# Moving the pace of layer 0 and the choice of engine for tanh rows in a two-layer attention kernel

## The chip, the cores and the metric

The kernel runs on one core of a Trainium2 chip. The metric is the device time of one execution in microseconds (us). The median of three runs of the kernel before is 5696.39 us (5690.69 to 5700.09).

## What is computed

The input x is 8 batches of 1024 tokens with 128 channels. Two layers follow each other.

```
# layer 0, 8 heads
q, k, v = x @ wq.T + bq, x @ wk.T + bk, x @ wv.T + bv
scores  = q . k / sqrt(128)                    # 1024 x 1024 for each batch and head; tokens (m, g) = 64 x 16
a       = softmax(softmax(scores, over m), over g)
x1      = layer_norm(a @ v @ wo.T + bo + x)
x2      = layer_norm(relu(x1 @ w1.T + b1) @ w2.T + b2 + x1)
# layer 1
B       = layer_norm(x2);  Wi = B @ W.T
s[i, j] = sum over d of v[d] * tanh(Wi[i, d] + Wi[j, d])
t       = x2 + softmax(s) @ B
out     = t + recurrence(layer_norm(t))        # y = sigmoid(wx_t + y @ V.T) along the tokens
```

Within a batch, layer 1 needs all of layer 0. Different batches are independent up to the recurrence, which takes its normalisation from all of them.

## The kernel before, in words

Everything but the opening loads and the closing recurrence is put down as a list of small operations, each with the engines that may do it and its cost there, its dependencies, and a priority (`pri`, a number: lower goes first). `Plan.emit` then plays the list through: it keeps a planned time for every engine, looks at the operations whose dependencies are planned, takes those that could start within 0.15 us of the earliest, and among these emits the one with the lowest sum of priority and the engine's own handicap. The instructions of each engine stand in the program in that order, which is fixed; on the chip an engine works through its own order and waits where it must. An operation that more than one engine may do goes to the one that wins this choice.

**Layer 0 of a batch** (`layer0(b)`) goes over 8 heads and, in a head, over 8 tiles of 128 queries. For each tile: scores on PE (L856), exponential on ACT (L859), sums over m and reciprocals on DVE (L863, L864), division on DVE (L867). For each pair of tiles: second exponential on ACT (L876, 2048 elements per partition), sums and reciprocals on DVE (L879, L880), division on GpSimd (POOL, L890), transposes on PE with copies by DVE (L770, L782), the product with the values on PE (L904) and its addition to zs on DVE (L909, L911). There are two score buffers (sc), two pairs of tile buffers (e) and two transposed buffers (aT). After the last head come a norm, the feed-forward matmuls (L944, L957) and another norm. The priority of a tile is its place on a pace line: `b - 1 - LEAD + STRETCH * (share of layer 0 done)`, with LEAD = 0.15 and STRETCH = 0.95 (1.25 for the last batch), so 64 tiles are 0.95/64 apart. In the first and last batch layer 0 is done in two halves of queries. In batch 0 nothing else is there to do beside it, and ACT may do evictions as well.

**Layer 1 of a batch** (`layer1(b)`) norms the tokens and projects them to wiT (L1085, copied by DVE, L782 and L1109). Scores are symmetric, so of the 8 x 8 blocks of 128 x 128 only the 36 on and over the diagonal are computed: row block `it` has `8 - it` of them. A *group* is one step of such a row block: tanh of the sums of `4k` tokens with all later ones, in one of five th buffers, and its product with v on PE (L1062, times_v). k is 1 for the wide row blocks 0 to 3, 2 for 4 and 5, and 4 and 8 for 6 and 7. A group can be filled in three ways:

- ACT alone: one activation per token with the token as bias (L999);
- POOL adds (L1009, four instructions over k tokens), then ACT makes one tanh of the whole buffer (L1045);
- DVE adds: row by row where k < 4 (L1003, with an accumulator output that nobody reads), or as POOL does where k >= 4 (L1009), then ACT's L1045.

The first operation of the group decides which engine fills it. The list `fillers` of `layer1` names the engines that may: for the wide row blocks ACT and POOL, and DVE in the last batch only. The priority of the rows of batch b goes from b to b + 0.222 (ROWS); their matmuls come LEAD ahead of that. The exponentials of the scores (L1158), transposes and the product with B (L1191) follow. The rest of layer 1 has priority b - 0.5. The parked outputs and wx go out and come back by SP's DMA queue.

The last stage is the recurrence (L1372 to L1381), and the transposed sums with the parked outputs.

```
def pace(n_part, h):
    return b - 1 - LEAD + STRETCH * (n_part * H + h) / (len(parts) * H)
...
ROWS = b + (past + n_blocks * s / 33) / len(E_first) / 4.5
L1 = ROWS - LEAD
```

Of the kernel before, what the change touches and what calls it, by code (L numbers as in the profile page):

```python
# [413 lines left out]
class Plan:  # L414
# [24 lines left out]
    def add(self, where, fn, r=(), w=(), pri=0, mode="full", take=None, give=None, behind=(), wait=(), port=False):  # L439
        n = len(self.ops)  # L440
        deps = set()
        for k in r:
            if k in self.writer:
                deps.add(self.writer[k])
        for k in (*w, *wait):
            if k in self.writer:
                deps.add(self.writer[k])
            deps.update(self.readers.get(k, ()))
        for k in w:
            self.writer[k] = n  # L450
            self.readers[k] = []
        for k in r:
            if k not in w:
                self.readers.setdefault(k, []).append(n)
        deps.discard(n)
        self.ops.append((where, fn, (pri, n), mode, deps, take, give, behind, port))
        self.by.append(None)
        return n
# [107 lines left out]
def fast_path(ctx: ExitStack, tc: tile.TileContext, a: dict, fits):  # L566
# [6 lines left out]
    NB, N, C = a["x"].shape  # L573
# [143 lines left out]
    add = plan.add  # L717


    LEAD, SOON, LATE = 0.15, 0.5, -0.3  # L720

    stats = ring("stat", 7, [P, 4, 9])

# [36 lines left out]
    def through_bank(pe, weight, r, evict, where, more, w, pri, choice=two):  # L760

        bank = Bank(*choice)
        n = len(plan.ops)
        add(("PE", weight), lambda _: pe(bank()), r=r, w=[("bank", n)], pri=pri, take=bank, wait=more + w)
        add(where, lambda e: evict(e, bank()), r=[("bank", n)] + more, w=w, pri=pri, give=bank)

    def transposes(srcs):
        def fn(bank):
            for i, s in enumerate(srcs):
                nc.tensor.transpose(bank[:, i * P : (i + 1) * P], s, ident)  # L770

        return fn

    def copy(dst):
        def fn(e, bank):
            src = bank
            if len(dst.shape) == 3:
                src = bank[:, : dst.shape[1] * P].rearrange("p (t c) -> p t c", c=P)
            if e == "ACT":
                nc.scalar.activation(dst, src, AF.Copy)  # L780
            else:
                nc.vector.tensor_copy(dst, src)  # L782

        return fn
# [4 lines left out]
    def layer0(b):  # L789
# [13 lines left out]
        def pace(n_part, h):  # L803
            return b - 1 - LEAD + STRETCH * (n_part * H + h) / (len(parts) * H)

        for n_part, part in enumerate(parts):
# [3 lines left out]
            for h in range(H):  # L810
                L0 = pace(n_part, h)
# [29 lines left out]
                for qt in qts:  # L841
                    L0 = pace(n_part, h + (qt - qts[0]) / len(qts))
# [30 lines left out]


                    ks = [("e", pair, q) for q in range(2)]
                    add(("ACT", 1.9), lambda _, e2=e2: nc.scalar.activation(e2, e2, AF.Exp), r=ks, w=ks, pri=L0)  # L876

                    def second_sums(_, e2=e2, r2=r2):
# [42 lines left out]
            L0 = b - 1 - SOON  # L921
# [53 lines left out]

    def group(it, at0, r0, k, wiT, all_wi, L1, ROWS, fillers, chain, left, both, first_half):

# [80 lines left out]
        def times_v(_):  # L1058
# [15 lines left out]
            ("PE", k * (1.69e-3 * (w - begin[0]) + 0.005 * n)), times_v, r=[("tanh", g)] + before,  # L1074
            w=[("sa", it, r0)] + after, pri=L1, mode="groups", give=slot,
        )
        return ("sa", it, r0)

    def projected(src, ks, w, use, kw, L1, bT, kb):

        through_bank(
            transposes([src[:, i, :] for i in range(4)]), 0.52, ks, copy(bT), ("DVE", 0.7), [], [kb], L1
        )
        through_bank(
            lambda bank: nc.tensor.matmul(bank, w, bT, start=True, stop=True), 0.9, [kb], *use, [], [kw], L1  # L1085
        )
# [8 lines left out]
    def layer1(b):  # L1095
        L1 = b - SOON
        X, kX = Xs[b % NX], ("X", b % NX)
        B, kB = Bs[b % 2], ("B", b % 2)
        wiT, kw = wiTs[b % 2], ("wiT", b % 2)

        early = b in (0, NB - 1)
        for qh in (1, 0) if early else (0, 1):
            Xg, kg = X[:, 4 * qh : 4 * qh + 4, :], kX + (qh,)
            Bg = B[:, 4 * qh : 4 * qh + 4, 0:C]
            layer_norm(Xg, kg, Bg, kB + (qh,), 6, L1)

            def numbered(_, bank, qh=qh):
                dst = wiT[:, 512 * qh : 512 * qh + 512]
                nc.vector.tensor_copy(dst.rearrange("p (t r c) -> p t r c", t=4, c=4), bank.rearrange("p (t c r) -> p t r c", t=4, c=4))  # L1109


            at = wiT[:, 512 * qh : 512 * qh + 512]
            projected(Bg, [kB + (qh,)], wa_sb, (numbered, ("DVE", 0.75)), kw + (qh,), L1, at, kw + (qh,))
        all_wi = [kw + (1,), kw + (0,)]

        E_at = E_first
        fills = [("fill", False), ("fill", True)]
        order = ((4,), (5, 7), (6,), (0,), (1,), (2,), (3,)) if early else shared  # L1120
        done, attended = set(), set()
        past = 0
        for pair in order:
            todo = []
            for it in pair:
                w = N - it * P
                k = max(1, N // w)
                wide = it < NT // 2
                for r0 in range(0, 32, k):
                    late = r0 + 3 * k >= 32  # L1130
                    if wide:
                        fillers = [("ACT", 0.0)] + ([] if late else [("POOL", 0.0)])
                        if b == NB - 1:
                            fillers += [("DVE", 0.1)]
                    elif it == NT // 2:
                        fillers = [("DVE", 0.1), ("ACT", 0.1)] + ([] if late else [("POOL", 0.0)])
                    else:
                        fillers = [("DVE", 0.1)] + ([("ACT", 0.1)] if early else [("POOL", 0.0)])
                    todo.append((r0 + 0.5 * (not wide), it, 0 if it == pair[0] else N - pair[0] * P, r0, k, fillers))
            left = {}  # L1140
            n_blocks = sum(NT - it for it in pair)
            keys = []
            for s, it, at0, r0, k, fillers in sorted(todo):
                ROWS = b + (past + n_blocks * s / 33) / len(E_first) / 4.5
                L1 = ROWS - LEAD
                keys.append(group(it, at0, r0, k, wiT, all_wi[:1] if early and pair[0] >= NT // 2 else all_wi, L1, ROWS, fillers, fills[it < NT // 2], left, fills if r0 == 0 else (), b == 0 and pair[0] >= NT // 2))
            past += n_blocks
            blocks = [("E", it, j) for it in pair for j in range(it, NT)]

            runs = [pair] if not early else [(it,) for it in pair]  # L1150

            def exps(_, runs=runs):
                at0 = 0
                for run in runs:
                    w = sum(NT - it for it in run)
                    Ep = E_sb[:, E_at[run[0]] : E_at[run[0]] + w, :].rearrange("p t (c r) -> p t c r", c=4)
                    S = sa[:, at0 : at0 + w * P].rearrange("p (t r c) -> p t c r", r=32, c=4)
                    nc.scalar.activation(Ep, S, AF.Exp)  # L1158
                    at0 += w * P

            add(("ACT", 0.2 * len(runs) + 0.833e-3 * n_blocks * P), exps, r=["sa"] + keys, w=blocks, pri=L1)
            for it in pair:
                D, kD = E_sb[:, E_at[it], :], ("E", it, it)
                add(("DVE", 0.28), lambda _, D=D: nc.vector.tensor_tensor(D, D, half, ALU.mult),
                    r=[kD], w=[kD], pri=L1, port=True)
                through_bank(
                    transposes([D]), 0.25, [kD],
                    lambda _, bank, D=D: nc.vector.tensor_tensor(D, bank[:, :P], D, ALU.add),
                    ("DVE", 0.3), [kD], [kD], L1,
                )  # L1170
            done.update(pair)
            for it in range(NT):
                if it not in attended and done.issuperset(range(it + 1)):
                    attended.add(it)
                    attention(b, it, X, kX, B, kB, E_at, L1)
# [67 lines left out]
    def check_bounds():  # L1243
# [73 lines left out]
        add(("DVE", 1.7), compared, r=[("at1", 0), ("at1", 1)] + [("ET", j) for j in range(1, NT)], w=["fits"], pri=LATE)  # L1317

    layer0(0)
    check_bounds()  # L1320
    for b in range(NB):
        if b + 1 < NB:
            load_xT(b + 1)
            layer0(b + 1)
        layer1(b)
# [139 lines left out]
```

## Time and profile before

| what | value |
|---|---|
| median of three runs | 5696.39 us |
| the profiled execution, its own time | 5699.62 us |
| its span, first to last instruction | 5697.8 us |
| mean granted clock of TensorE | 0.975 |
| PE busy | 5166.6 us (91%) |
| ACT busy | 5263.0 us (92%) |
| DVE busy | 4754.1 us (83%) |
| POOL busy | 4186.4 us (73%) |
| rows of one batch, first L1062 to the next batch's first, batches 1 to 4 | 680, 679, 679, 674 us |
| last feed-forward matmul of layer 0 of batch 7 (L957) | ends at 5184 us |
| last matmul of the rows of batch 7 | starts at 5601 us |

PE is TensorE's matmuls, PEld its weight loads, DVE is VectorE, ACT ScalarE, POOL GpSimd. Busy shares are averages over stages that differ: an opening of some 400 us with layer 0 of batch 0, a long stage in which layer 0 of batch b + 1 runs beside the rows of batch b, the rows of batch 7 alone, and some 97 us of recurrence and output. Durations of instructions that follow each other closely overlap, so start-to-start distances are shorter than the durations. The ends of matmuls are modelled, so a busy PE is not a PE at its peak.

### The profile page before, as it was taken

What the parts mean: (1) busy time and instruction counts of PE and PEld (TensorE: products, weight loads), DVE (VectorE), ACT (ScalarE), POOL (GpSimd) and SP (SyncE); (2) the same over time, 40 slices, a digit from 0 to 9 for tenths busy, and PEclk for the clock granted to TensorE, in tenths of its full rate; (3) what the DMA queues carried; (4) which work ended last, traced back from release to release, by engine and by line L of the source; (5) the groups of instructions that cost most, each with busy time, mean ns of one, the idle gap of its engine ahead of it and who ended that gap; (6) DMA issues with size and microseconds to landing.
All of it is one profiled execution on the core that took longest, in us unless ns stands there. A gap on an engine that the chain in (4) does not pass through costs nothing.

```text
span 5697.8 us, 97791 instructions
## 1 busy us (share of the span) xinstructions
PE 5166.6 (91%) x39013; PEld 2765.7 (49%) x39013; DVE 4754.1 (83%) x7545; ACT 5263.0 (92%) x4964; POOL 4186.4 (73%) x2678
## 2 busy tenths in 40 slices
PE   8899999899989999899998999989998999987567
PEld 6555455455544555445454455445454445543125
DVE  7989676778996889968898689986899669999886
ACT  5499999999998999899998999989998999999994
POOL 2362997788877888588796888868887886882882
PEclk9999999999999999999999999999999999998988
DMA  2000000000000000000000000000000000000001
GB/s 60 1 5 1 1 1 5 8 1 1 1 5 8 1 1 1 8 5 1 1 5 5 5 1 1 5 8 1 1 1 3 7 1 1 1 21 14 1 1 64
DMA packets 27330, 37.82 MB, mean 7 GB/s; under 512 B 2464, under 2 KB 19232, under 8 KB 26864
## 3 DMA queue, kind: packets, MB, share of 16 engines
q1 hardware_dynamic: 24832, 27.99, 1.5%
q8 instruction: 308, 5.05, 0.4%
q10 hardware_dynamic: 1872, 3.16, 0.2%
q14 instruction: 158, 1.29, 0.1%
q0 software_dynamic: 160, 0.33, 0.1%
HBM read 19.41 MB, written 12.06 MB: 6 GB/s over the span
## 4 chain that ended last, share of the span: by engine, by line
PE 40%; DVE 24%; ACT 23%; issue 4%; POOL 1%; DMA 0%; DVEq 0%; ACTq 0%; POOLq 0%
PE sa L1062 16%; ACT th L1045 10%; ACT th L999 9%; PE m L904 8%; PE sc L856 6%; PE m L770 4%; DVE th L1003 3%; DVE stat_e L879 3%; DVE th L1009 3%; DVE stat_e L863 2%; DVE aT L782 2%; ACT wx L876 2%; DVE wx L867 2%; ACT sc L859 2%; PE m L1191 1%
## 5 line engine op out<-in xcount | busy, mean ns | idle before, releaser
L1009 POOL TENSOR_TENSOR th<-wiT 128x896 f32<-128x896 f32 (+55 forms) x2088 | 3131.7, 1535 | 436.8 <-PE sa L1062 400.4
L1062 PE MATMUL sa<-th,vpat 128*32 128x512 f32 (+27 forms) x24576 | 2104.4, 466 | 223.6 <-ACT th L1045 212.6
L999 ACT ACTIVATE th<-wiT 128x516 f32<-128x516 f32 (+55 forms) x3044 | 2203.1, 798 | 37.1 <-DVE wiT L1109 21.1
L1045 ACT ACTIVATE th<-th 128x4096 f32<-128x4096 f32 (+54 forms) x766 | 2083.8, 2746 | 49.0 <-DVE th L1003 28.0
L890 POOL TENSOR_TENSOR wx<-wx,stat_e 128x1024 f32<-128x1024 f32 x512 | 998.3, 1971 | 755.9 <-DVE stat_e L880 527.5
L1062 PEld LDWEIGHTS sa<-th,vpat 128*32 128x32 f32 x24576 | 674.8, 111 | 1470.4 <-issue 834.4
L856 PE MATMUL sc<-xT,wx 128*128 128x512 f32 x2048 | 985.7, 606 | 36.0 <-DVE wx L867 35.8
L904 PE MATMUL m<-aT,wx 128*128 128x256 f32 x3584 | 862.2, 389 | 14.7 <-DVE aT L782 12.0
L1003 DVE TENSOR_SCALAR_CACHE_REDUCE th<-wiT 128x384 f32<-128x384 f32 (+47 forms) x1092 | 758.1, 694 | 86.3 <-PE sa L1062 15.0
L904 PEld LDWEIGHTS m<-aT,wx 128*128 128x128 f32 x3584 | 660.7, 191 | 238.9 <-issue 89.9
L782 DVE COPY aT<-m 128x512 f32<-128x512 f32 x927 | 598.2, 672 | 138.6 <-PE m L770 136.2
L863 DVE TENSOR_REDUCE stat_e<-sc 128x16 f32<-128x1024 f32 x512 | 620.1, 1211 | 101.1 <-ACT sc L859 99.9
L879 DVE TENSOR_REDUCE stat_e<-wx 128x128 f32<-128x2048 f32 x256 | 583.2, 2278 | 102.5 <-ACT wx L876 101.8
L867 DVE TENSOR_TENSOR wx<-sc,stat_e 128x1024 f32<-128x1024 f32 x512 | 623.4, 1218 | 23.8 <-DVE stat_e L864 0.5
L770 PE MATMUL m<-ident,wx 128*128 128x128 f32 x3932 | 571.9, 280 | 56.7 <-DVE aT L782 29.3
L770 PEld LDWEIGHTS m<-ident,wx 128*128 128x128 f32 x3932 | 434.9, 141 | 357.6 <-issue 164.2
L859 ACT ACTIVATE sc<-sc 128x1024 f32<-128x1024 f32 x512 | 513.1, 1005 | 92.3 <-PE sc L856 76.6
L876 ACT ACTIVATE wx<-wx 128x2048 f32<-128x2048 f32 x256 | 486.8, 1902 | 90.8 <-DVE wx L867 90.8
L856 PEld LDWEIGHTS sc<-xT,wx 128*128 128x128 f32 x2048 | 357.3, 192 | 367.1 <-issue 301.7
L1009 DVE TENSOR_TENSOR th<-wiT 128x1024 f32<-128x1024 f32 (+28 forms) x280 | 392.1, 1439 | 3.9 <-PE sa L1062 3.0
L880 DVE RECIPROCAL stat_e<-stat_e 128x128 f32<-128x128 f32 x256 | 243.9, 953 | 8.8
L738 POOL TENSOR_TENSOR stat<-stat,neg_half 128x4 f32<-128x4 f32 x64 | 65.3, 1020 | 245.4 <-DVE stat L735 230.6
(169 smaller groups left out, 3055.5 us busy)
## 6 DMA issues: line engine op xcount, KB each, us to landing
xT<-in_xt_dram SPq DMA_DIRECT2D x8, 512.0 KB, 3.7
th<-in_x_dram SPq DMA_DIRECT2D x8, 512.0 KB, 7.5
parked<-X SPq DMA_DIRECT2D x16, 256.0 KB, 2.3
xr<-parked SPq DMA_DIRECT2D x8, 512.0 KB, 8.3
parked_wx<-bT SPq DMA_DIRECT2D x14, 256.0 KB, 2.0
wx<-parked_wx SPq DMA_DIRECT2D x7, 512.0 KB, 3.3
out_dram<-ot ACTq DMA_DIRECT2D x8, 256.0 KB, 2.1
out_dram<-ot SPq DMA_DIRECT2D x8, 256.0 KB, 2.2
```

The lines of the kernel that those rows point to most:

```text
L770: nc.tensor.transpose(bank[:, i * P : (i + 1) * P], s, ident)
L856: nc.tensor.matmul(sc[:, cols], u[:, qt * P : (qt + 1) * P], xT[:, cols], start=True, stop=True)
L863: nc.vector.tensor_reduce(r1, sc.rearrange("p (m g) -> p g m", g=G), AX.X, ALU.add)
L867: nc.vector.tensor_tensor(e3, sc3, r1.unsqueeze(1).to_broadcast([P, M, G]), ALU.mult)
L879: nc.vector.tensor_reduce(r2, e2.rearrange("p q (m g) -> p q m g", g=G), AX.X, ALU.add)
L890: nc.gpsimd.tensor_tensor(e3, e3, r2[:, q, :].unsqueeze(2).to_broadcast([P, M, G]), ALU.mult)
L904: nc.tensor.matmul(bank()[:, :256], vp[:, t, :], aT[:, t, :], start=t == 0, stop=t == NT - 1)
L999: nc.scalar.activation(rows(c)[:, r, :], wiT[:, i0 + begin[c] :], AF.Tanh, bias=w_i(c, r))
L1003: nc.vector.tensor_scalar(rows(c)[:, r, :], wiT[:, i0 + begin[c] :], w_i(c, r), 0.0, ALU.add, ALU.add, accum_out=unused)
L1009: eng.tensor_tensor(rows(c), wiT[:, i0 + begin[c] :].unsqueeze(1).to_broadcast(shape), w_i(c).unsqueeze(2).to_broadcast(shape), ALU.add,)
L1045: lambda _: nc.scalar.activation(slot()[:, : at[4]], slot()[:, : at[4]], AF.Tanh),
L1062: nc.tensor.matmul(sa[32 * c : 32 * c + 32, s:s1], vpat[:, 31 - r0 - r : 63 - r0 - r], rows(c)[:, r, s - at0 - begin[c] : s1 - at0 - begin ...
```

## The change

Three edits. LEAD in the pace of layer 0 goes from 0.15 to 0.35; the matmuls of the rows keep 0.15 as a literal. From the second exponential of a pair on, the operations of that pair in layer 0 take a priority that is lower by DOWN = 0.06. And in the fillers of the wide row blocks DVE is named, with a handicap of 0.1, in all batches and not in the last alone.

```diff
-    LEAD, SOON, LATE = 0.15, 0.5, -0.3
+
+    LEAD, DOWN, SOON, LATE = 0.35, 0.06, 0.5, -0.3
...
                     ks = [("e", pair, q) for q in range(2)]
+                    L0 -= DOWN
                     add(("ACT", 1.9), lambda _, e2=e2: nc.scalar.activation(e2, e2, AF.Exp), r=ks, w=ks, pri=L0)
...
                     if wide:
-                        fillers = [("ACT", 0.0)] + ([] if late else [("POOL", 0.0)])
+                        fillers = [("ACT", 0.0)] + ([] if late else [("POOL", 0.0)]) + ([("DVE", 0.1)] if b < NB - 1 else [])
                         if b == NB - 1:
                             fillers += [("DVE", 0.1)]
...
                 ROWS = b + (past + n_blocks * s / 33) / len(E_first) / 4.5
-                L1 = ROWS - LEAD
+                L1 = ROWS - 0.15
```

## The prediction

> **What bounds the kernel now.** I read first the busy times by stage: the opening (layer 0 of batch 0 alone), the overlapped stage to 5184 us (last layer-0 matmul of batch 7), and the rest (attention of batch 7 alone, then the recurrence). Columns: PE, PEld, DVE, ACT, POOL busy, then PE clock and DMA.
>
> ```profile
> 0.00:400.00 400.00, 367.96 (x1757) 246.07 (x1757) 340.40 (x447) 254.31 (x395) 166.10 (x102) 1.00 0.08 23
> 400.00:5184.00 4784.00, 4465.93 (x34077) 2368.55 (x34080) 3995.95 (x6194) 4579.86 (x4232) 3720.87 (x2367) 0.98 0.01 4
> 5184.00:5698.00 514.00, 332.66 (x3185) 151.09 (x3177) 417.79 (x907) 428.87 (x339) 299.42 (x209) 0.89 0.05 19
> ```
>
> In the long stage ACT is busy 4580 of 4784 us (95.7%), PE 93.3%, DVE 83.5%, POOL 77.8%. So ACT bounds it, with 204 us of idle time. Next I asked where that idle time lies: three windows inside the steady part (the first, fourth and last line), and two at a change of batch.
>
> ```profile
> 1300.00:1600.00 300.00, 289.20 (x2345) 157.80 (x2344) 269.26 (x407) 294.01 (x247) 249.76 (x169) 0.99 0.00 1
> 1640.00:1780.00 140.00, 115.91 (x787) 61.72 (x786) 120.89 (x250) 109.82 (x116) 81.11 (x49) 0.93 0.02 7
> 2290.00:2450.00 160.00, 136.16 (x943) 77.66 (x943) 144.47 (x295) 125.05 (x137) 90.34 (x59) 0.94 0.03 9
> ...
> 4800.00:5100.00 300.00, 277.10 (x2247) 144.98 (x2247) 286.73 (x573) 293.32 (x258) 244.30 (x171) 1.00 0.02 5
> ...
> 600.00:900.00 300.00, 290.82 (x1925) 148.58 (x1924) 202.21 (x246) 300.00 (x239) 271.94 (x164) 1.00 0.00 1
> ```
>
> Steady, ACT runs at 98 to 100%. At a change of batch it idles 30 us in 140 and 35 us in 160; the windows 2960 to 3100, 3650 to 3790 and 4290 to 4430 lose another 18, 17 and 15 us. PE and POOL fall there too. The ACT timeline of the first change, then ACT's list of waits in the long stage, say why:
>
> ```profile
> 1728.86 2.86 ACT L1045 ACTIVATE th<-th 128x3188 f32<-128x3188 f32 x1 [2.79 <-DVE th L1003]
> 1734.62 0.60 ACT L1158 ACTIVATE E<-sa 128x512 f32<-128x512 f32 x1 [2.90 <-PE sa L1062]
> 1746.60 1.91 ACT L876 ACTIVATE wx<-wx 128x2048 f32<-128x2048 f32 x1 [11.38 <-DVE wx L867]
> 1751.18 1.15 ACT L999 ACTIVATE th<-wiT 128x1024 f32<-128x1024 f32 x1 [2.66 <-DVE wiT L1109]
> ...
> 1753.17 10.42 ACT L999 ACTIVATE th<-wiT 128x1024 f32<-128x1024 f32 x10
> ```
>
> ```profile
> ACT wx L876 <- DVE wx L867: 75.4, 26, 11.4
> ACT sc L859 <- PE sc L856: 36.0, 29, 7.5
> ACT th L999 <- DVE wiT L1109: 21.1, 5, 15.6
> ```
>
> The rows of the old batch are used up at 1734; those of the new one need wiT, which comes only at 1751, behind layer 0's FFN and norms. Between, ACT has almost nothing. Last, the groups that the change touches:
>
> ```profile
> L999 ACT ACTIVATE th<-wiT 128x516 f32<-128x516 f32 (+55 forms) x3044 | 2203.1, 798 | 37.1 <-DVE wiT L1109 21.1 <-PE sa L1062 15.4
> ...
> L1003 DVE TENSOR_SCALAR_CACHE_REDUCE th<-wiT 128x384 f32<-128x384 f32 (+47 forms) x1092 | 758.1, 694 | 86.3 <-PE sa L1062 15.0 <-DVE th L1003 6.6 <-issue 0.9
> ...
> L1009 DVE TENSOR_TENSOR th<-wiT 128x1024 f32<-128x1024 f32 (+28 forms) x280 | 392.1, 1439 | 3.9 <-PE sa L1062 3.0 <-ACT th L999 0.9
> ```
>
> **What the Trainium skill says.** "ScalarE: Activation LUTs", What ACT_TABLE_LOAD costs: 280 ns + 0.833 ns per element with a pointer bias, 186 ns without, and about 93 ns of overlap back to back. The trace agrees: the ten 1024-element rows above take 1.042 us each from start to start, and four batched tanh of 4096 elements from 5243.56 us take 14.02 us, 3.505 each. "Perfetto Trace Analysis", Optimizing Scalar/DVE Operations: GpSimd shares an SBUF port with DVE, and a two-port DVE operation holds it. The trace fits: L742 on X, of 128 elements, takes 248 to 2087 ns. L1003's durations lie tight on one line (1.28 us at 1024 elements, 83 ns more for its accumulator read), so I take it as not contending. Same page, Optimization Strategy: interleave regimes whose busiest engine differs; the windows above show two such regimes.
>
> **The change, part by part.** Counts come from both built programs.
>
> *DVE as a filler of wide rows.* In batches 0 to 6 the wide groups go from ACT 515, POOL 381, DVE 0 to 388, 292, 216. POOL's free time goes to narrow groups: POOL 83 to 173, DVE 146 to 62, ACT 79 to 73. Batch 7 barely moves. In instructions: L999 3044 to 2444, L1045 766 to 903, L1003 1092 to 1760, DVE L1009 280 to 60, POOL L1009 unchanged at 2088.
> ACT: elements are the same. At 0.835 ns per element (fitted to the durations of both kinds), a row carries 1.042 - 0.855 = 0.187 us of overhead, a batched tanh 3.505 - 3.420 = 0.085. So -600 x 0.187 + 137 x 0.085 = -112 + 12 = -100 us.
> DVE: the added L1003 rows are mostly wide ones. The widths of both programs, at 1.053 ns per element and 0.215 us of overhead a row (fitted to this trace's rows, accumulator read included), give +804 us; 220 L1009 fewer at 392.1/280 = 1.40 us give -308. Net +496 us.
>
> *LEAD 0.35 for layer 0's pace.* It issues nothing new. In the planned order, layer 0 of batch b used to end with 94 to 100% of batch b-1's rows done, now (batches 1 to 6) with 77 to 86% done. After the last wiT copy of a batch there stood 15, 0, 0, 1, 1, 1 ACT tanh of the old batch; now 48 to 101. The waits for wiT (21 us) and most of the idle time at the changes of batch (115 us in five windows, two not counted) get cover. The loads on SP's queue keep their own priority and stay ahead of need. For batch 7, layer 0 used to end with 18.4% of its own rows done, now 3.5%: 0.149 x 36 blocks = 5.4 blocks move into the last stage. Rows 0 to 3 there take 359 us for 26 blocks (5242 to 5601), 13.8 us each: +74 us there, ACT -72 and DVE -63 us in the long stage.
>
> *DOWN 0.06.* Second exponential, sums, POOL division, transposes and matmuls of a begun pair go ahead of up to four later tiles (0.06 over a pace of 0.95/64 a tile). No instruction is added; queued behind them are the next tiles' scores and first exponential. Gain at most the 75 us of waits on L867, loss at most another 36 us like those for the scores; I take 0.
>
> *The sum.* Long stage after: ACT 4580 - 100 - 72 = 4408 us; DVE 3996 + 496 - 63 = 4429; PE 4466 - 5.4 x 8.5 (221.5/26) = 4420. Three engines now carry the same load, so the stage's length is that load over the share at which they can run together. Bounds: 98.0% (ACT in 1300 to 1600) gives 4519; 95.6% (DVE in 4800 to 5100, the stage with all four busy) gives 4633; PE's best 300 us, 600 to 900, is 96.9%. Below 94.0% (4429/4710) nothing is gained. I take 96.5%: 4590. With the opening kept at 400 (it holds none of the new rows) and the end at 514 + 74 = 588, the span is 5578, 120 under 5697.8. The execution's own time was 5699.6, so 5580; the runs shown have a median 3 us lower: **5577 us**.
>
> **The rivals.**
> 1. *Forecast, 0.55*: 5577, own range 5525 to 5635.
> 2. *The new rows are only a filler, 0.15*: DVE takes one only when idle, so it never bounds, and changes of batch become like 1300 to 1600. 4429/0.98 = 4519, so 5506. For it: DVE at 86% in the last stage with ACT at 96 to 100%. Against: PE would have to be busy 97.8%, above its best window.
> 3. *Chain delays eat most of it, 0.18*: layer 0's sums and divisions stand behind 1.28 us rows in DVE's queue, and DVE and ACT reach 95.0%: 4662, so 5649. For it: 102 us in which DVE's second sums (L879) wait for ACT's exponential, 75 us in which ACT waits for L867.
> 4. *DVE becomes the bound, slower, 0.12*: the order on DVE is fixed, and each of 216 wide groups puts four rows, some 4 us, ahead of work on which ACT's exponential, POOL's division and PE's evictions wait. From an occupancy under 94.0% it loses; at 93% the stage is 4762 and the time 5749. For it: no 300 us of the trace have DVE above 95.6%; the two-port norms would meet a busier POOL (at 1005 ns, as on ET, instead of 794 and 558 ns: +56 us). Against: the replaced L1009 were the port-bound kind, and the planner takes DVE rows with a 0.1 handicap.
>
> That the change does nothing is excluded: the orders differ from the first layer-0 tiles on.
>
> **From these to the numbers.** Some 0.2% (11 us) is what a measurement of this kernel can tell from no change. Faster: all of 1 and 2, most of 3: 0.84. Same: 0.05, from the border of 3 and 4. Slower: 0.11. The range leaves out the best of 2 (under 5495) and most of 4: 5495 to 5690.
>
> **What would show it.** Right: ACT tanh of the old batch running while wiT of the new one is copied, no ACT wait on L1109 above some us; ACT busy near 5160 us in all, DVE near 5250 (92 to 94% of the span); PE clock near 1.0 at the changes of batch; the end from the last layer-0 matmul some 70 us longer. Wrong: ACT's waits on L867, or PE's on DVE L782, growing past 200 us with DVE above 95% everywhere (rival 4), or the idle time at the changes of batch still there.

## The result, and the profile after

The changed kernel takes 5683.69 us (median of 20 runs, 5677.29 to 5689.71), the kernel before 5696.27 in the same sessions: a ratio of 0.9977 (95% interval 0.9971 to 0.9984). It is faster by 0.23%, where 2.1% was forecast. The changed kernel's line numbers are one higher from L721 on and two higher from L878 on.

First the stages of the changed kernel, cut at the same events as before the change (PE, PEld, DVE, ACT, POOL busy, PE clock, DMA). The last layer-0 matmul of batch 7 now ends at 5065 us.

```profile
0.00:400.00 400.00, 363.18 (x1703) 242.67 (x1704) 342.94 (x449) 244.62 (x389) 152.79 (x94) 1.00 0.08 23
400.00:5065.00 4665.00, 4372.39 (x33559) 2360.69 (x33561) 4378.88 (x7036) 4414.00 (x3673) 3618.98 (x2361) 0.98 0.01 4
5065.00:5680.00 615.00, 387.14 (x3756) 175.00 (x3748) 508.40 (x1181) 513.66 (x438) 321.68 (x224) 0.87 0.05 17
```

The loads came as forecast: in the long stage ACT 4414 us (4408 forecast), DVE 4379 (4429), PE 4372 (4420). The lengths did not. The long stage takes 4665 us instead of 4590, so ACT is busy 94.6% of it, less than the 95.7% before the change; the end takes 615 instead of 588. These two, 75 and 27 us, are the whole miss of 102 us in the span (5680 for 5578).

Next, what ACT waited for over the whole run, longest first:

```profile
ACT sc L860 <- PE sc L857: 88.2, 74, 18.2
ACT th L1001 <- PE sa L1064: 83.2, 49, 8.7
ACT th L1047 <- DVE th L1005: 79.0, 56, 6.8
ACT wx L878 <- DVE wx L868: 71.4, 33, 10.4
```

and the same waits in the kernel before, again over the whole run:

```profile
ACT wx L876 <- DVE wx L867: 90.8, 35, 11.4
ACT sc L859 <- PE sc L856: 76.6, 54, 8.1
ACT th L1045 <- DVE th L1003: 28.0, 24, 2.8
ACT th L999 <- DVE wiT L1109: 21.1, 5, 15.6
ACT th L999 <- PE sa L1062: 15.4, 10, 4.5
```

The waits for wiT, 21 us before, are gone from the list, as forecast. But rows done by ACT now wait 83 us for a th buffer that PE has yet to finish with (15 before), batched tanh 79 us for DVE's rows (28), scores 88 us (77). The waits for the division (L868) became shorter. In the long stage alone the same four waits went from 15 to 80, from 15 to 51, from 36 to 49 and from 75 to 46 us. New waits have taken the place of the old idle time: ACT idles 251 us of the long stage (4665 - 4414), where it was 204.

One of them can be read off instruction by instruction. These are the changed kernel's ACT, PE, DVE and POOL timelines around 1030 us, a change of batch (start, length, instruction, in brackets the idle time ahead of it):

```profile
1045.23 1.01 ACT L860 ACTIVATE sc<-sc 128x1024 f32<-128x1024 f32 x1 [18.15 <-PE sc L857]
...
1035.83 1.11 PE L771 MATMUL m<-ident,B 128*128 128x128 f32 x4 [6.94 <-DVE aT L783]
1036.74 5.83 PE L906 MATMUL m<-aT,wx 128*128 128x256 f32 x16
...
1030.79 4.38 DVE L743 TENSOR_SCALAR B<-X,stat 128x128 f32<-128x128 f32 x4
1035.10 1.28 DVE L783 COPY aT<-m 128x512 f32<-128x512 f32 x2
...
1053.19 3.83 POOL L892 TENSOR_TENSOR wx<-wx,stat_e 128x1024 f32<-128x1024 f32 x2 [18.36 <-DVE stat_e L882]
```

Four norm steps hold DVE for 4.38 us, after 3.2 us of sums and reciprocals; the two copies of aT stand behind them; PE waits 6.94 us for the copies, then does a long product first; the scores that ACT needs come behind that, and ACT stands still for 18 us. POOL, done at 1035, waits as long. Each engine keeps to its written order while another is late.

### The profile page after: what moved, and what is told of

Read it like the earlier page. It is cut to its first block, busy times and chain, and to the rows that moved or that the text cites. A ratio compares the mean times of both kernels' runs of the same rounds, so it can differ in the third digit from the quotient of the medians.

```text
span 5679.7 us, 98799 instructions
## 1 busy us (share of the span) xinstructions
PE 5122.7 (90%) x39013; PEld 2778.3 (49%) x39013; DVE 5230.2 (92%) x8664; ACT 5172.3 (91%) x4498; POOL 4093.4 (72%) x2678
## 4 chain that ended last, share of the span: by engine, by line
PE 48%; DVE 30%; ACT 16%; issue 5%; POOL 1%; DMA 0%; DVEq 0%; ACTq 0%; SPq 0%; POOLq 0%
PE sa L1064 18%; PE m L906 10%; PE sc L857 8%; ACT th L1047 8%; DVE th L1005 7%; PE m L771 5%; ACT th L1001 5%; DVE stat_e L881 4%; DVE wx L868 3%; DVE stat_e L864 3%; DVE aT L783 3%; ACT wx L878 2%; PE m L835 1%; DVE stat_e L882 1%; ACT sc L860 1%
## 5 line engine op out<-in xcount | busy, mean ns | idle before, releaser
L1011 POOL TENSOR_TENSOR th<-wiT 128x1024 f32<-128x1024 f32 (+58 forms) x2088 | 3056.6, 1499 | 676.9 <-PE sa L1064 645.5
L1047 ACT ACTIVATE th<-th 128x3072 f32<-128x3072 f32 (+50 forms) x903 | 2496.1, 2795 | 86.4 <-DVE th L1005 79.0
L1064 PE MATMUL sa<-th,vpat 128*32 128x512 f32 (+34 forms) x24576 | 2079.0, 468 | 254.0 <-ACT th L1047 232.5
L1001 ACT ACTIVATE th<-wiT 128x398 f32<-128x398 f32 (+60 forms) x2444 | 1692.1, 764 | 84.3 <-PE sa L1064 83.2
L1005 DVE TENSOR_SCALAR_CACHE_REDUCE th<-wiT 128x288 f32<-128x288 f32 (+50 forms) x1760 | 1550.4, 881 | 159.4 <-PE sa L1064 44.5
L892 POOL TENSOR_TENSOR wx<-wx,stat_e 128x1024 f32<-128x1024 f32 x512 | 982.3, 1941 | 701.2 <-DVE stat_e L882 526.0
L906 PE MATMUL m<-aT,wx 128*128 128x256 f32 x3584 | 845.1, 389 | 10.1 <-DVE aT L783 8.7
L906 PEld LDWEIGHTS m<-aT,wx 128*128 128x128 f32 x3584 | 676.8, 193 | 196.5 <-issue 42.8
L868 DVE TENSOR_TENSOR wx<-sc,stat_e 128x1024 f32<-128x1024 f32 x512 | 623.5, 1218 | 23.9 <-DVE stat_e L865 0.5
L771 PEld LDWEIGHTS m<-ident,wx 128*128 128x128 f32 x3940 | 448.4, 142 | 362.9 <-issue 169.7
L878 ACT ACTIVATE wx<-wx 128x2048 f32<-128x2048 f32 x256 | 486.9, 1902 | 71.9 <-DVE wx L868 71.4
L835 PEld LDWEIGHTS m<-Wvo,xT 128*128 128x128 f32 x1080 | 133.9, 193 | 58.0 <-issue 22.2
```

Source lines behind the costliest of these rows:

```text
L868: nc.vector.tensor_tensor(e3, sc3, r1.unsqueeze(1).to_broadcast([P, M, G]), ALU.mult)
L892: nc.gpsimd.tensor_tensor(e3, e3, r2[:, q, :].unsqueeze(2).to_broadcast([P, M, G]), ALU.mult)
L906: nc.tensor.matmul(bank()[:, :256], vp[:, t, :], aT[:, t, :], start=t == 0, stop=t == NT - 1)
L1001: nc.scalar.activation(rows(c)[:, r, :], wiT[:, i0 + begin[c] :], AF.Tanh, bias=w_i(c, r))
L1005: nc.vector.tensor_scalar(rows(c)[:, r, :], wiT[:, i0 + begin[c] :], w_i(c, r), 0.0, ALU.add, ALU.add, accum_out=unused)
L1011: eng.tensor_tensor(rows(c), wiT[:, i0 + begin[c] :].unsqueeze(1).to_broadcast(shape), w_i(c).unsqueeze(2).to_broadcast(shape), ALU.add,)
```

## The experiments

Two theories to begin with: A, DVE's new rows crowd layer 0's chain on DVE; B, the earlier pace puts layer 0 ahead of the rows' matmuls on PE. Each of the three edits was done alone, and DVE's rows and DOWN were also undone one at a time. The change without LEAD was not run.

**Parts of the change.**

```diff
# lead_only and lead_down: LEAD 0.35, rows' matmuls with the literal 0.15
-    LEAD, SOON, LATE = 0.15, 0.5, -0.3
+    LEAD, DOWN, SOON, LATE = 0.35, 0.0, 0.5, -0.3      # lead_down: DOWN 0.06, with L0 -= DOWN
# down_only: LEAD stays 0.15, DOWN 0.06; dve_only: only DVE in the fillers of the wide row blocks
```

> Only LEAD 0.35 for layer 0's pace. Theory A (the new DVE rows crowd layer 0's chain on DVE and so eat the gain): without them the earlier pace keeps its gain at the changes of batch, about 5640 us. Theory B (the earlier pace puts layer 0 ahead of the rows' matmuls on PE, th buffers come free later and ACT waits for them instead of for wiT; the work moved to the front is given back at the end): no gain, 5685 to 5705 us, with ACT's L999 waiting for PE some 60 us or more (15 us before) and wiT no longer waited for.

> Only DOWN 0.06 for begun pairs. Both theories: within 15 us of 5696, no more than a reshuffle of waits between the scores and the second exponential on ACT. If it is the part that moves ACT's wait for scores (36 us before, 88 us after the whole change), that wait shows here at 70 us or more.

> Only DVE as a filler of wide rows in all batches. Theory A (DVE rows crowd layer 0's chain): no faster, 5695 to 5720 us, since the changes of batch stay as they are and DVE comes to some 92% busy. Theory B (the earlier pace is what loses): ACT has some 100 us less to do and bounds the long stage, so 5620 to 5650 us.

> LEAD 0.35 and DOWN 0.06, without DVE rows in batches 0 to 6. Theory A: 5620 to 5640 us, clearly faster than the whole change. Theory B: 5685 to 5705 us, no faster than before.

| kernel | median, us | ratio to before (95%) |
|---|---|---|
| lead_only | 5709.26 | 1.0016 (1.0007 to 1.0024) |
| down_only | 5734.69 | 1.0061 (1.0048 to 1.0075) |
| dve_only | 5695.88 | 0.9993 (0.9984 to 1.0001) |
| lead_down | 5707.48 | 1.0015 (1.0008 to 1.0022) |

No part gains alone. What theory A forecast did not come: without DVE's rows the earlier pace took 5709 and 5707 us, not 5640 or less. What theory B forecast did not come either: DVE's rows alone left the time where it was, and in lead_only ACT's rows waited 27 us for PE, not 60 or more. down_only lost 35 us, which neither theory had. (Its expectation sets 36 us of waits for scores, a figure of the long stage, beside 88, one of the whole run. Over the whole run it was 77 before, 88 after the whole change and 109 in down_only.) These are single orders, and further below orders with the same intention differ by more than these parts do; so the times alone refute neither theory.

The page of dve_only and its ACT waits show what DVE's rows do without the earlier pace:

```profile
PE 5152.9 (91%) x39013; PEld 2773.3 (49%) x39013; DVE 5207.4 (91%) x8825; ACT 5143.8 (90%) x4409; POOL 4204.8 (74%) x2782
```

```profile
ACT sc L859 <- PE sc L856: 103.8, 63, 8.6
ACT th L999 <- DVE wiT L1109: 99.5, 5, 45.0
```

ACT has 119 us less to do (5144 for 5263), and gives it back in waits, most of all for wiT (21 us before, 99.5 now): the rows are done sooner, but layer 0 of the next batch is not. That the two edits need each other was then tried with the kernel that has both, without DOWN:

> LEAD 0.35 and DVE rows in all batches, without DOWN 0.06. DOWN alone lost 35 us, but beside LEAD alone it cost nothing (5709 and 5707 us). If DOWN is a loss that the other two parts cover: 5650 to 5672 us, faster than the whole change. If it costs nothing here either: 5675 to 5690 us. If the DVE rows need it, since it moves the begun pairs ahead of them: 5692 us or more.

It took 5669.87 us, 0.9953 (0.9940 to 0.9967): 29 us under the kernel before, where the two alone sum to +6, and 14 us under the whole change, which was measured in another session.

**Is one engine the bound?** Here the written order stays as it is, and one engine gets some 215 us less to do. If its load set the time, the time would follow.

```diff
# pe_light
-                        for t in range(4 * part, 4 * part + 4):
+                        for t in ((0, 1, 3), (4, 6, 7))[part]:
# act_light
-... nc.scalar.activation(e2, e2, AF.Exp)
+... nc.scalar.activation(e2[:, :, : N // 2], e2[:, :, : N // 2], AF.Exp)
# dve_light
-                        nc.vector.reciprocal(r2, r2)
+                        nc.vector.reciprocal(r2[:, :, 0:1], r2[:, :, 0:1])
```

> The kernel before, its order unchanged; layer 0's product with the values leaves out 2 of its 8 key tiles (t = 2 and 5), so PE has some 980 records of 0.215 us, 211 us, less to do. If PE is what bounds: 5490 to 5560 us. If ACT bounds, as the prediction had it: within 30 us of 5697. If no engine bounds, but the coupling of layer 0's chain with the rows under a fixed order: 5600 to 5660 us.

> The kernel before, its order unchanged; the second exponential leaves out half of its columns (256 x 0.853 us), so ACT has 218 us less to do. If ACT bounds: 5480 to 5560 us. If PE bounds: within 30 us of 5697. If the coupling bounds: 5600 to 5660 us.

> The kernel before, its order unchanged; the reciprocals of the second sums are made for 2 of 128 columns only, so DVE has some 215 us less to do (256 x 0.84 us) and each pair's chain is shorter by 0.84 us. If PE or ACT bounds: within 30 us of 5697. If the coupling bounds: 5620 to 5670 us, of which part is the shorter chain.

> The changed kernel, its order unchanged; layer 0's product with the values leaves out 2 of its 8 key tiles, PE has 211 us less to do. If PE bounds: 5480 to 5550 us. If DVE and ACT bound it since the change: within 30 us of 5684. If the coupling bounds: 5590 to 5650 us.

> The changed kernel, its order unchanged; half of the columns of the second exponential left out, ACT has 218 us less to do. If ACT is what bounds since the change: 5480 to 5560 us. If PE is (its chain share rose from 40 to 48%, ACT's fell from 23 to 16%): less than before the change, 5655 to 5675 us.

> The changed kernel, its order unchanged; reciprocals of the second sums for 2 of 128 columns, DVE has some 215 us less to do. If DVE has become the bound: 5480 to 5560 us. If it only carries a larger share of the chain (30% for 24% before): 45 to 65 us under the changed kernel, 5620 to 5640 us. If it is not on the path: 5660 us or more.

> The kernel before, its order unchanged, with both cuts at once: 2 of 8 key tiles left out of the product with the values (PE 211 us less) and half the columns of the second exponential left out (ACT 218 us less). Alone they gave 15.5 and 38 us. If PE and ACT are both all but critical, each hiding what the other frees: far more than the sum, 5560 to 5610 us. If the two are small independent shares of one chain of waits: the sum, 5640 to 5650 us.

> The kernel before, its order unchanged, with three cuts at once: 2 of 8 key tiles left out of the product with the values (PE 211 us less), half the columns of the second exponential (ACT 218 us less), and the second reciprocals made for 2 of 128 columns (DVE 215 us less). Alone 15.5, 38 and 36 us; PE and ACT together 89. If the three engines are co-critical, each covering the others: well over 125 us (89 + 36), 5500 to 5550 us. If what is left is waiting that no engine's work sets: 5565 to 5585 us, the sum.

> The changed kernel, its order unchanged, with the same three cuts at once. Alone 31, 26 and 39 us, together 96 us if they add. If the three engines are co-critical, and more so than before the change: 5480 to 5540 us, 145 us or more under the changed kernel. If they only add: 5580 to 5595 us.

| less work on | kernel before: us, gain | changed kernel: us, gain |
|---|---|---|
| PE, 211 us | 5682.27, 16 | 5652.59, 31 |
| ACT, 218 us | 5659.90, 38 | 5658.07, 26 |
| DVE, 215 us | 5661.46, 36 | 5644.27, 39 |
| PE and ACT | 5609.63, 89 | not run |
| all three | 5524.66, 175 | 5502.08, 182 |

(Gains are against the kernel before in the same session, 5697.82 to 5699.72, or against 5683.69, from a session in which the kernel before took 5696.27. The ratio of the last row to the kernel before is 0.9698, 0.9682 to 0.9714, and 0.9657, 0.9641 to 0.9673.)

The amounts in the first column were worked out ahead. In the traces of the single cuts the busy time fell by 135 us on PE, 199 on ACT and 182 on DVE in the kernel before, and by 149, 197 and 167 in the changed one. On PE the product itself took 209 us less in before_pe_light, but the rows' matmuls (L1062) took 2168.5 us instead of 2104.4, with the mean granted clock at 0.969 instead of 0.975.

So no engine alone is worth more than a quarter of what its trace was relieved of. All three together are worth 80 and 83% of the largest amount worked out ahead, about twice the sum of the single gains. That is what three engines critical together would do, in both kernels: when one is freed, the others still hold the time. The chain that ended last shows the hand-over, in the kernel before, then in before_act_light, then in before_pe_light:

```profile
PE 40%; DVE 24%; ACT 23%; issue 4%; POOL 1%; DMA 0%; DVEq 0%; ACTq 0%; POOLq 0%
```

```profile
PE 51%; DVE 27%; ACT 9%; issue 3%; POOL 1%; DMA 0%; DVEq 0%; POOLq 0%; ACTq 0%
```

```profile
ACT 32%; PE 27%; DVE 26%; issue 6%; POOL 1%; DMA 0%; DVEq 0%; ACTq 0%; SPq 0%; POOLq 0%
```

The first of these lines was on the page from the start: PE and DVE each held as large a share of the chain as ACT, or a larger one. One rival is not excluded: all three cuts lie in the same chain of a pair in layer 0 (exponential, reciprocals, product), so each shortens that chain as well as its engine's load. No run in an unchanged order took work from an engine outside it.

**How much is the luck of an order?** The parts differ by 10 to 35 us. The pace was therefore shifted by 0.01 on either side of both kernels, which leaves the plan's intention as it is but makes the planner write another order, and give some groups of rows to another engine.

```diff
-    LEAD, SOON, LATE = 0.15, 0.5, -0.3                 # before_lead14, before_lead16
+    LEAD, SOON, LATE = 0.16, 0.5, -0.3                 # or 0.14; the rows' matmuls keep 0.15
-    LEAD, DOWN, SOON, LATE = 0.35, 0.06, 0.5, -0.3     # after_lead34, after_lead36
+    LEAD, DOWN, SOON, LATE = 0.36, 0.06, 0.5, -0.3     # or 0.34
```

> A control: the kernel before with 0.16 for 0.15 in layer 0's pace alone, a change that means nothing for the pace (0.01 of a batch) but makes the planner choose another order. If the orders of such neighbours differ by luck alone as much as the parts of the change do (10 to 35 us): 5 us or more off 5697 on either side. If an order's time is a smooth matter of its parameters: within 4 us of it.

> The same control on the changed kernel: 0.36 for 0.35 in layer 0's pace. If luck of the order is as large as the parts' effects: 5 us or more off 5684 on either side, perhaps 15. If not: within 4 us of it.

> The other neighbour of the kernel before: 0.14 for 0.15 in layer 0's pace. If an order's luck is worth some 50 us and the order of the kernel before is a fortunate one: 5715 to 5745 us, like its neighbour at 0.16 (5745). If 0.16 was the odd one: 5690 to 5705 us.

> The other neighbour of the changed kernel: 0.34 for 0.35. If the order of the changed kernel is an unfortunate one: 5630 to 5665 us, like its neighbour at 0.36 (5635). If 0.36 was the odd one: 5680 to 5695 us.

| pace | kernel before: us, ratio (95%) | pace | changed kernel: us, ratio (95%) |
|---|---|---|---|
| 0.14 | 5730.02, 1.0055 (1.0038 to 1.0071) | 0.34 | 5600.60, 0.9828 (0.9812 to 0.9845) |
| 0.15 | 5696.27, 1 | 0.35 | 5683.69, 0.9977 (0.9971 to 0.9984) |
| 0.16 | 5745.39, 1.0080 (1.0063 to 1.0097) | 0.36 | 5634.51, 0.9885 (0.9869 to 0.9902) |

An order's luck is worth up to 83 us between neighbours. The kernel before is the best of its three, the changed kernel the worst of its own; still the two ranges, 5696 to 5745 and 5601 to 5684, do not overlap, and their means, 5724 and 5640, lie 84 us apart. The forecast was 119 us. The neighbour at 0.34 is faster than both kernels, by 1.7% and 1.5%. lead_dve, at 5670, falls among the changed kernels. All runs together: the four orders that have both the earlier pace and DVE's rows took 5601 to 5684 us, the seven that lack one or both 5696 to 5745. That the two edits gain together, and neither alone, rests on this comparison more than on any single pair.

The long stages of after_lead34 and before_lead16, the best and the worst of the six, are these:

```profile
400.00:4996.00 4596.00, 4353.86 (x33546) 2360.86 (x33545) 4322.53 (x6953) 4421.69 (x3719) 3608.57 (x2351) 0.98 0.01 4
```

```profile
400.00:5232.00 4832.00, 4492.13 (x34051) 2389.78 (x34049) 3951.94 (x6069) 4575.66 (x4190) 3737.84 (x2379) 0.98 0.01 4
```

| pace | 0.14 | 0.15 | 0.16 | 0.34 | 0.35 | 0.36 |
|---|---|---|---|---|---|---|
| ACT busy in the long stage, us | 4577 | 4580 | 4576 | 4422 | 4414 | 4405 |
| length of the long stage, us | 4817 | 4784 | 4832 | 4596 | 4665 | 4630 |
| ACT's share | 95.0% | 95.7% | 94.7% | 96.2% | 94.6% | 95.1% |

ACT's work is nearly the same within each family, and 154 to 175 us lower in the changed one (172 forecast). The share changes with the order: one point of it is 49 us. The work of the other engines is not quite the same: at 0.34 DVE has 56 us less to do in the long stage than at 0.35 (43 of them over the run in the rows of L1005, 64 rows fewer), and is as full, 94.0% and 93.9%. How much of the 69 us between these two comes from that, and how much from waits, was not separated.

The means of the three orders put the change's two terms apart: the long stage goes from 4811 to 4630 us, 181 less (194 forecast), and the end from 513 to 608, 95 more (74 forecast). Three orders on each side are few. The same 100 us of the run, first in the changed kernel, then in after_lead34, is one place where the two part (ACT 71 against 99.5 us busy):

```profile
1000.00:1100.00 100.00, 87.40 (x658) 53.03 (x654) 92.75 (x158) 71.41 (x62) 61.12 (x48) 0.93 0.00 1
```

```profile
1000.00:1100.00 100.00, 97.14 (x821) 54.20 (x814) 94.58 (x170) 99.52 (x87) 84.21 (x67) 1.00 0.01 1
```

## Why the prediction was wrong

*What bounds the kernel.* "So ACT bounds it" was wrong. Relieving ACT (218 us as worked out, 199 in the trace) in the unchanged order gave 38; the like on DVE, which was busy only 83.5%, gave 36, on PE 16, and on all three 175. A busy share of 95.7% beside PE at 93.3% named the busiest engine, not the bound.

*DVE as a filler.* Right in its terms: ACT 91 us less over the run (5263.0 to 5172.3; 100 forecast), DVE 476 more (496). As time, the one order that has it alone (dve_only) shows no gain; the orders that have it with the earlier pace are all faster than those without.

*LEAD.* Right that the waits for wiT go. Wrong that the idle time at the changes of batch would go with them: ACT's idle time in the long stage rose from 204 to 251 us, as waits for th buffers, for DVE's rows and for the scores.

*DOWN.* Taken at 0. Alone it measured +35 us, beside LEAD -2, beside LEAD and DVE's rows +14. Neighbouring orders differ by more, so no value for it is shown; nor is one for LEAD or DVE's rows alone.

*The sum.* The step that failed is "I take 96.5%", the share at which the three loaded engines can run together: 94.6% was measured, with the loads as forecast, and the long stage took 4665 us instead of 4590. That one number stood for a share that went from 94.6 to 96.2% over the three orders of the changed kernel, 69 us of the long stage; the trace of one execution could not show that, and neighbouring orders had to be run. By these few orders, some 62 of the 75 us are such differences: the kernel before lies 27 us below the mean of its three long stages, the changed kernel 35 above. At 0.34 the long stage was 4596 us, and the forecast of it would have stood; that would have been luck too. Most of the signs named for being right came (no waits for wiT, ACT at 5172 us, DVE at 5230): they told of the loads, not of the share.

Rival 3 came nearest. Its 95.0% gave a long stage of 4662, and what parts its 5649 from 5684 is mostly the end. Its cause, layer 0's sums and divisions behind DVE's rows, is not shown: ACT's waits for the division fell from 75 to 46 us, and without DVE's rows (lead_down) the time was no better.

*The end.* A term that was mis-sized: 5.4 blocks more, priced at the 13.8 us of the wide row blocks, +74 us. What is left at the end first is the narrow row blocks. In the changed kernel the 8.7 narrow blocks that remain at 5065 us (96.5% of 36, less the 26 wide ones) last to 5231, 19 us each; 5.4 of them would be 103 us, and +101 was measured. The fit is in part chance: those 166 us also hold the last attention of batch 6 (64 matmuls of L1193 after 5065; before the change none came after 5184). Row blocks 5 to 7, from 5122 on and nearly free of it, took 109 us for 6 blocks, 18 each (98 us before the change, with the end of layer 0 beside them). Why they are slow is argued, not tried: POOL may not fill row blocks 5 to 7 in the last batch, and it was busy 1 us between 5100 and 5200, with PE at 54%, since no layer 0 is left.

*Rival 4*, DVE as the bound, did not come: DVE was at 93.9% of the long stage, just under the 94.0% where the prediction saw no gain, and relieving it (167 us in the trace) gave 39.

*Readings.* Three figures of the prediction are slightly off, without weight for the result. The 10.42 us of ten rows run to the end of the last one; from start to start a row took 1.033 us and a batched tanh 3.478, which makes ACT's term -99. And there are 300 us with DVE at 96.2% (from 4078.6) and with PE at 97.3% (from 1236.1), so 95.6 and 96.9% were not the best of the trace.

What stays open: why one order is luckier than another. The stop at 1030 us is one case; whether the chip's durations that differ from the planner's costs (the four norm steps took 1.1 us each, planned at 0.35) are what spoils an order was not tried. Nor was a change that takes work from an engine outside layer 0's chain, or one that lets POOL fill the narrow row blocks at the end.

## What to carry to other kernels

When several engines are nearly full (here 83 to 96% of the long stage), ask which of them share the chain that ended last, and test by lightening one, then all, in an unchanged order, before pricing a gain by the busiest one. Where a planner writes the order, run a few neighbours of a parameter on both sides of a change: a comparison of two single orders tells of their luck as much as of the change. Price work that is moved to another stage by what that very work costs there, not by the stage's average.

## What was not expected of the hardware

The order alone, with ACT's work in the long stage within 4 us in one family and 17 us in the other, moved that stage by 48 us and 69 us (DVE's work differed by 53 and 56 us). And a norm step on DVE, with POOL busy beside it, took 1.1 us where its shortest instance in the kernel before took 0.25.
